# A cross-network kernel on one core: the first tile on two queues, a small product moved forward, and fewer pooling passes

## The chip, the cores and the metric

The kernel runs on one core of one Trainium2 chip. A core has a matrix engine (TensorE, "PE" in the profile; its weight loads are the row "PEld"), three engines for elementwise work (VectorE "DVE", ScalarE "ACT", GpSimd "POOL") and a queueing engine (SyncE, "SP"). SP, ACT and POOL can issue DMA transfers. The metric is the device time of one execution in microseconds; less is better.

## The reference

The reference is a compressed interaction network for recommendation, in float32. The input `x` has 1024 examples of 64 features by 16 embedding elements.

```python
x0 = h = x
for i in range(3):
    z = einsum('bfe,bge->bfge', x0, h).reshape(B, 64 * 64, e)
    y = einsum('oc,bce->boe', W[i], z) + b[i]
    x_i, h = (y[:, :64], y[:, 64:]) if i < 2 else (y, y)
    xs.append(x_i)
pooled = sum(concatenate(xs, axis=1), axis=2)
out = pooled @ fc_w.T + fc_b
```

Each layer forms all products of a feature of `x` with a feature of `h` and contracts them with weights; the last step pools over the 16 elements and weighs the channels to one number for each example. Since that step is linear, the kernel needs the third layer only through one weighted sum of its weights. So it builds a matrix "M" on the chip: layer 3's weights are summed with `fc_w` into `v2`, and M is `v2` times layer 2's upper weights. From M come the "Q weights", with which the same products z give a factor that is multiplied with `h` and pooled.

## The kernel before, in words

The work is cut into 32 chunks of 32 examples. A chunk's `x` is a tile of 512 columns (32 examples by 16 elements). The engine on the two sides of a product works on shifted copies of x: `xa` holds x with the features turned by 0 to 3 rows (4 slices, index i), `xb` holds x turned by multiples of 4 (4 quarters, index j). A product tile z for (j, i) is `xa[i] * xb[j]`, made by DVE or POOL (`product`, L239, whose instruction has line L243), and each z is contracted by TensorE with a 128 by 64 slice of `w_all`.

The program is written with a manual schedule: each engine runs its instructions in the order of the text, and semaphores are waited for where data is needed. The first four chunks ("head", c0 to c3, in the order 2, 3, 0, 1) run straight in program order; what follows is a list of operations with due times, sorted at L1075.

The order of the head is this.

- ACT issues the DMA of `vs` (L103), a tile of 128 by 196 with biases, factors and a column of `fc_w`. ACT makes `fv2` from it (L108), the weights of the `pv` matmuls.
- TensorE runs seven matmuls on zeros into the scratch bank `misc` (L113-114).
- SP issues x of c0 and the layer-1 weights slice by slice (L193-197; the instruction of `load_xa` has line L145), x of c1 (L198), layer 3's weights `w2t` (L202), layer 2's `w1h` (L203, L206), and c2's tiles.
- TensorE makes the shifted quarters of c0 and c1 by multiplying the first x slice with 0/1 matrices (`shift_pair`, L221, tiles "xp"). DVE, POOL and ACT make products and weights slice by slice; TensorE contracts c0 (L260).
- c1 is contracted in quarters by `half_contract` (L251). Between its quarters TensorE computes `pv` (L369), which DVE turns and ACT and DVE copy to `v2t` (L374 to L384).
- M is four matmul groups `pm` (L398) and a small one `pcx` (L407). ACT copies M to SBUF (L409). M is written to DRAM tile `md` by six DMAs (L421-431: two at L422, one each at L425, L426, L427, L428), on SP and one on ACT, and read back in two skewed patterns (L472, L478). `q_weights` (L505, DVE) adds both into the Q weights.
- c2 and c3 are contracted by L251, then `head_q_tile` (L284) contracts c0 and c1 with the Q weights.
- `linear` (L351-354) is a row of 384 numbers broadcast to 128 partitions by one DMA on SP. POOL multiplies parts of it (L456), DVE sums it (L969), into the constant of the output.

After the head, pairs of chunks follow the list of due times (matmuls at L536, products at L650 and L667). At the end, `acc` holds for each chunk pair k two parts of the pooled sums: part 0 from the factors, part 1 from `x_v0x`. `add_parts` (L1028) adds them for all pairs but k = 1, the last one, `pools` (L1034) sums over partitions by small matmuls `pool` (L952; the weights are two columns "ones") into `po`, and `finish` (L959) adds the constant and writes the result. The pair k = 1 is completed last, with weights `turned` that swap the two halves, and its last columns have a bank `pl` of their own.

Of the kernel before, what the change touches and what calls it, by code (L numbers as in the profile page):

```python
# [38 lines left out]
AF = mybir.ActivationFunctionType  # L39
# [7 lines left out]
N = CB * E  # L47
H2 = N // 2
CUT = 24
NCH = B // CB  # L50
NI = 4
NJ = 4
NT = NI * NJ
XR = 128 + NI
# [6 lines left out]
QS = 16.0  # L61
# [9 lines left out]
def cin_kernel(ctx, tc, xra, xrb, wh, w0r, w1h, w2t, wx1, wx0, vec, lin, out):  # L71
    nc = tc.nc
# [8 lines left out]
    def const_tile(name, shape):  # L81
        return const.tile(shape, F32, tag=name, name=name)
# [9 lines left out]
    def used(n, times=1):  # L92
        left[n] -= times
        assert left[n] >= 0
        if left[n] == 0:
            vacant.append(n)
# [3 lines left out]


    vs = const_tile("vs", [128, NV])
    nc.scalar.dma_start(out=vs, in_=vec)  # L103
    fc2, bh1, bh2 = vs[:, 0:1], vs[:, 1:2], vs[0:64, 2:3]
    fcb, w0ds, fcr = vs[:, 3:4], vs[:, 4:68], vs[:, 68:196]

    fv2 = const_tile("fv2", [128, 32])
    nc.scalar.activation(fv2, fc2.to_broadcast([128, 32]), AF.Identity, scale=QS)  # L108

    misc = ps.tile([128, N], F32, tag="acc", name="misc", bufs=4)  # L110

    zeros = nc.const_aps.tensor(0.0, [128, 128])
    for n in (128,) * 6 + (64,):  # L113
        nc.tensor.matmul(misc[:, 0:n], zeros, zeros[:, 0:n], start=True, stop=True)

    shift = const_tile("shift", [128, 96])
# [1 line left out]
    for base in (0, 64, -64):  # L118
        nc.gpsimd.affine_select(
            out=shift, in_=shift, compare_op=ALU.not_equal, fill=1.0, base=base,  # L120
# [18 lines left out]

    xas, xbs, xxs, es = {}, {}, {}, {}  # L140

    def load_xa(c, at=slice(0, NI)):
        if c not in xas or at.start == 0:
            xas[c] = xp.tile([128, NI, N], F32, tag="xa", name=f"xa_{c}")
        nc.sync.dma_start(  # L145
            out=xas[c][:, at, :],
            in_=bass.AP(
                tensor=xra.tensor, offset=c * XR * N + at.start * N,
                ap=[[N, 128], [1, (at.stop - at.start) * N]],
            ),  # L150
        )

    def quarter(c, j):
        xbs.setdefault(c, {})[j] = xp.tile([128, N], F32, tag="xb", name=f"xb_{c}_{j}", bufs=9)
        return xbs[c][j]
# [26 lines left out]
    def load_chunk(c):  # L182
        load_xa(c)
        load_xb(c)

    c0, c1, c2, c3 = HEAD
# [4 lines left out]
    w1b = take()  # L191
    w1s = flat(w1b)
    for i in range(NI):  # L193
        load_xa(c0, slice(i, i + 1))
        nc.sync.dma_start(out=w0t[:, i, :], in_=wh if i == 0 else w0r[:, i - 1, :])
        if i == 0:
            load_xa(c1, slice(0, 1))
    load_xa(c1, slice(1, 4))  # L198
    w0s = [w0t[:, i, :].rearrange("p (j v g) -> p j v g", v=2, g=F) for i in range(NI)]
    xb_gps = [quarter("gps", n) for n in range(3)]  # L200
    for k in range(2):
# [30 lines left out]
    acc = const_tile("acc", [128, 2, NCH // 2, CB])  # L232
# [15 lines left out]
    def half_contract(c, *js, last=None):  # L248
        for j in js:
            for i in range(NI):  # L250
                nc.tensor.matmul(  # L251
                    accs[c][halves[i % 2]], w_all[:, j * NI + i, 0:64], blocks[zs[c, j]][:, i, :],
                    start=(j == 0 and i < 2), stop=(j == last and i > 1),
                )
            used(zs[c, j])
# [12 lines left out]
    def keep_h1(c):  # L268
        if c != c0:
            h, k = halves[c % 2], c // 2  # L270
            nc.scalar.activation(hb[h, k, :], accs[c][halves[0]], AF.Identity, bias=bh1[halves[0]])
            nc.scalar.copy(snaps[k][h], accs[c][halves[1]])
            return
        for n in range(2):
            nc.scalar.activation(
                hb[halves[c % 2], c // 2, n * H2 : (n + 1) * H2], accs[c][halves[n]],
                AF.Identity, bias=bh1[halves[n]],
            )
# [53 lines left out]
    for i in range(NI):  # L332
# [15 lines left out]
    new_acc(c1)  # L348

    load_chunk(c3)  # L350
    linear = const_tile("linear", [128, 384])  # L351
    nc.sync.dma_start(
        out=linear, in_=bass.AP(tensor=lin.tensor, offset=lin.offset, ap=[[0, 128], [1, 384]])
    )
    keep_h1(c0)
    for j in (3, 2):
        product(c1, j, engine=nc.gpsimd)
# [8 lines left out]
    for n in range(2):  # L366
        pv = ps.tile([128, 512], F32, tag=("set", "y")[n], name=f"pv2_{n}")
        for k in range(4):
            nc.tensor.matmul(  # L369
                pv[32 * k : 32 * k + 32], fv2, w2s[n][:, k * 512 : (k + 1) * 512],  # L370
                start=True, stop=True,
# [9 lines left out]
    for h in range(2):  # L381
        at = slice(32 * h, 32 * h + 32)
        nc.vector.tensor_copy(v2t[halves[h], at], v2q[halves[h]])
        nc.scalar.copy(v2t[halves[1 - h], at], v2q[halves[h]])  # L384
    used(v2b)
    half_contract(c1, 1, 2, last=2)


    mb = take()
# [15 lines left out]
    pcx = ps.tile([128, 1], F32, tag="acc", name="pcx", bufs=4)  # L405
    for to in halves:
        nc.tensor.matmul(pcx[to], v2t[0:64], bh2, start=True, stop=True)  # L407
    for m in (0, 2, 1, 3):
        nc.scalar.copy(m_sb[:, m, :], pms[m])  # L409

# [5 lines left out]
    def m_ap(f1, f2, dims):  # L416
        return bass.AP(tensor=md.tensor, offset=md.offset + f1 * row + f2 * F, ap=dims)
# [3 lines left out]
    for half, queue in enumerate((nc.sync, nc.scalar)):  # L421
        queue.dma_start(  # L422
            out=m_ap(0, 32 * half, [[row, F], [1, 32 * F]]), in_=m_rows[halves[half]]
# [4 lines left out]
    nc.sync.dma_start(  # L428
        out=m_ap(64, 68, [[row, 4], [4 * F, 7], [1, 4 * F]]),
        in_=m_rows[0:4, 4 * F :].rearrange("p (k c) -> p k c", c=4 * F),  # L430
    )
    used(mb)

# [35 lines left out]
    queues = (nc.sync, nc.scalar)  # L469
# [47 lines left out]
    turned = const_tile("turned", [128, 2])  # L517
    for n in range(2):
        nc.gpsimd.memset(turned[halves[n], n : n + 1], 0.0)
        nc.gpsimd.memset(turned[halves[n], 1 - n : 2 - n], 1.0)  # L520
    nc.gpsimd.memset(acc[:, 0, 1, CUT:], 0.0)


    ops = []
# [1 line left out]
    def at(when, fn, *args, **flags):  # L526
        ops.append((when, len(ops), fn, args, flags))

    def zipped(when, *columns):
        for n, column in enumerate(columns):  # L530
            for m, job in enumerate(column):
                if job is not None:
                    at(when + m + n / len(columns), *job)
# [387 lines left out]
    for n, p in enumerate(pairs):  # L921
        t = T0 + SPAN * n
# [23 lines left out]
    NP = NCH // 2  # L946
    QP = NP // 4
# [4 lines left out]
    def pool(k0, k1, part=0, rows=ones, **flags):  # L952
        g, at = k0 // QP, slice(k0 % QP, (k1 - 1) % QP + 1)
        nc.tensor.matmul(  # L954
            po[0][32 * g : 32 * g + 2, at, :], rows, acc[:, part, k0:k1, :],
            tile_position=(0, 32 * g), skip_group_check=True, **flags,
        )

    def finish(k0, k1, queue):  # L959
        g, at = k0 // QP, slice(k0 % QP, (k1 - 1) % QP + 1)  # L960
        rows = slice(32 * g, 32 * g + 2)
        nc.scalar.activation(
            res[rows, at, :], po[0][rows, at, :], AF.Identity, bias=cst[rows]
        )
        queue.dma_start(out=outs[:, k0:k1, :], in_=res[rows, at, :])
# [14 lines left out]
    t, q = T0 + SPAN * NPAIR, pairs[-1]  # L980
    first, cuts = slice(0, CUT), (slice(0, E * CUT), slice(E * CUT, N))
# [32 lines left out]
    def end_uu(n):  # L1014
        cols = cuts[n]
        nc.vector.scalar_tensor_tensor(
            uu[:, 0, cols], ends[n], 1.0 / QS, snaps[3][:, cols], ALU.mult, ALU.mult
        )
# [6 lines left out]
    def quarters():  # L1025
        return [(0, 1), (2, QP)] + [(n, n + QP) for n in range(QP, NP, QP)]
# [5 lines left out]
        po.append(ps.tile([128, QP, CB], F32, tag="set", name="po"))  # L1032

    def pools():  # L1034
        for m in quarters():
            pool(*m, start=True, stop=True)
        pool(1, 2, 1, start=True, stop=False)
        for m in quarters():
            finish(*m, nc.sync)

# [8 lines left out]
    for when, c in ((-5, 2), (0, 3)):  # L1049
# [11 lines left out]
    at(t - 0.7, end_squares)  # L1061
    at(t + 9.9, end_h)
    at(t + 13.6, x_v0x, 1)
    at(t + 13.7, sums, 1, of=slice(1, 2))
    t += 23
    at(t - 8, add_parts)
    at(t - 0.2, end_uu, 0)
    at(t - 0.1, sums, 1, of=slice(0, 1), half=first)
    zipped(
        t,  # L1070
        *[[(end_q, c, m, 1) for m in range(NT)] + [(end_extra, c, 1)] for c in (3, 2)]
    )
    at(t + 8, pools)

    for when, n, fn, args, flags in sorted(ops, key=lambda op: op[:2]):  # L1075
# [2 lines left out]

    last = cuts[1]
    end_uu(1)  # L1080
    pool(1, 2, rows=turned, start=False, stop=True)
    pl = ps.tile([2, N - E * CUT], F32, tag="acc", name="pl", bufs=4)
    nc.tensor.matmul(pl, ones, uu[:, 1, last], start=True, stop=False)
    nc.tensor.matmul(
# [81 lines left out]
```

## Time and profile before

| what | value |
|---|---|
| three runs of the kernel before | 445.19, 444.74, 446.3 us (median 445.19) |
| the profiled execution | 444.88 us |
| its span, first to last instruction | 443.1 us |
| TensorE busy | 439.6 us (99%) |
| DVE busy | 402.2 us (91%) |
| POOL busy | 373.5 us (84%) |
| ACT busy | 117.7 us (27%) |
| first x tile landed | 4.05 us |
| last instruction of the output's DMA issue | 440.90 us |

Times inside the trace count from the first instruction of the span. A row of the timeline gives start, length, engine, line, operation, output tile and inputs, and the count of merged instructions, then the idle time of the engine before it and what ended it. A float32 matmul stands in the trace as two passes, so the seven matmuls on zeros are 14 rows. Matmuls on different parts of the array start together: a pair of 64-column matmuls, or four of 64 by 64, share one time slot. The ends of matmuls are modelled, so the distance from start to start tells the pace. The chain of work follows the end back through what released each step.

### The profile page before, as it was taken

To read this page: it belongs to the slowest core of one execution; us is meant where nothing else is said; L and a number is where in the kernel's file an instruction comes from. 1 tells how busy PE (TensorE), PEld (TensorE's weight loads), DVE (VectorE), ACT (ScalarE), POOL (GpSimd) and SP (SyncE) were. 2 spreads that over 40 slices of the span, in tenths; PEclk is the share of its full clock that TensorE was granted. 3 is DMA by queue.
4 is the path that set the end of the run, shared out by engine and by line. 5 is a ranking of instruction groups with operands and counts; after the bars stand their busy time and mean duration, and the time that the engine had idled before them with its cause. 6 is when DMAs were issued, how large, how long until landed. Compare 5 with 4: busy or idle time off the path is not lost.

```text
span 443.1 us, 5949 instructions
## 1 busy us (share of the span) xinstructions
PE 439.6 (99%) x2234; PEld 160.8 (36%) x2234; DVE 402.2 (91%) x305; ACT 117.7 (27%) x216; POOL 373.5 (84%) x136
## 2 busy tenths in 40 slices
PE   9999999999999999999999999999999999999997
PEld 5333344336533333333333333333333333333345
DVE  4896899999998999999999999999999999999744
ACT  3164341242412123131312314131231313123211
POOL 4916799999998979899898979989798997989900
PEclk9999999999999999999999999999999999999999
DMA  8998997399769756896849868597568958592400
GB/s 302 409 342 189 353 410 308 105 337 240 268 135 328 180 190 233 185 332 125 300 140 254 269 163 300 125 333 185 185 233 183 347 120 288 189 272 66 89 1 0
DMA packets 35204, 99.85 MB, mean 225 GB/s; under 512 B 6404, under 2 KB 7204, under 8 KB 28712
## 3 DMA queue, kind: packets, MB, share of 16 engines
q1 hardware_dynamic: 31704, 84.70, 53.9%
q0 software_dynamic: 1872, 13.63, 16.8%
q10 hardware_dynamic: 1600, 1.15, 1.1%
q8 instruction: 17, 0.28, 0.3%
q14 instruction: 11, 0.09, 0.1%
HBM read 84.20 MB, written 1.64 MB: 194 GB/s over the span
## 4 chain that ended last, share of the span: by engine, by line
PE 98%; DMA 1%; DVE 0%; issue 0%
PE alpha L536 43%; PE delta L536 23%; PE beta L536 11%; PE acc L536 7%; PE acc L251 5%; PE q L536 3%; PE acc L284 3%; PE acc L260 2%; PE xp L221 1%; DMA xa<-in_xra 1%; PE y L536 0%; PE pv L369 0%; PE pm L398 0%; PE hx L536 0%; PE po L954 0%; DVE hb L1091 0%
## 5 line engine op out<-in xcount | busy, mean ns | idle before, releaser
L667 POOL TENSOR_TENSOR z<-z,z 128x2048 f32<-128x2048 f32 (+1 forms) x85 | 300.2, 3576 | 24.4 <-PE alpha L536 13.9
L650 DVE TENSOR_TENSOR z<-xa,xp 128x2048 f32<-128x2048 f32 x103 | 231.3, 2280 | 2.9 <-ACT xp L564 1.0
L536 PE MATMUL alpha<-z,ws 128*64 128x512 f32 x624 | 233.3, 593 | 0.0
L536 PEld LDWEIGHTS alpha<-z,ws 128*64 128x64 f32 x624 | 74.5, 137 | 89.5 <-issue 81.9
L536 PE MATMUL delta<-z,w_all 128*64 128x512 f32 x208 | 96.4, 592 | 0.0
L536 PE MATMUL alpha<-z,w_all 128*64 128x512 f32 x208 | 92.4, 592 | 0.0
L536 PE MATMUL beta<-z,w_all 128*64 128x512 f32 x208 | 91.7, 594 | 0.0
L536 PE MATMUL delta<-z,ws 128*64 128x512 f32 x208 | 91.4, 592 | 0.0
L564 ACT COPY xp<-xb 128x512 f32<-128x512 f32 x88 | 51.4, 586 | 130.0 <-DVE z L650 112.9
L243 DVE TENSOR_TENSOR z<-xa,xp 128x2048 f32<-128x2048 f32 (+2 forms) x29 | 43.3, 1546 | 3.1 <-ACT xp L564 2.0
L536 PEld LDWEIGHTS alpha<-z,w_all 128*64 128x64 f32 x208 | 28.5, 137 | 29.1 <-issue 28.0
L536 PEld LDWEIGHTS delta<-z,w_all 128*64 128x64 f32 x208 | 28.5, 137 | 28.7 <-issue 27.4
L536 PEld LDWEIGHTS delta<-z,ws 128*64 128x64 f32 x208 | 28.5, 137 | 28.7 <-issue 27.4
L243 POOL TENSOR_TENSOR z<-xa,xb 128x2048 f32<-128x2048 f32 x6 | 27.2, 4553 | 13.6 <-DMA xb<-in_xrb 13.5
L536 PEld LDWEIGHTS beta<-z,w_all 128*64 128x64 f32 x208 | 28.0, 137 | 27.4 <-issue 25.7
L536 PE MATMUL acc<-z,w_all 128*64 128x512 f32 x128 | 28.2, 592 | 0.0
L681 ACT ACTIVATE snap<-alpha,vs 64x512 f32<-64x512 f32 x13 | 8.9, 683 | 52.1 <-PE alpha L536 52.1
L251 PE MATMUL acc<-z,w_all 128*64 128x512 f32 x96 | 21.4, 596 | 0.0
L308 DVE TENSOR_REDUCE acc<-uu 128x64 f32<-128x1024 f32 (+2 forms) x19 | 19.6, 1036 | 0.2
L684 ACT COPY snap<-delta 64x512 f32<-64x512 f32 x13 | 7.6, 581 | 42.2 <-PE alpha L536 27.7
L656 DVE TENSOR_TENSOR xp<-xp,xb 128x512 f32<-128x512 f32 x26 | 18.1, 697 | 0.6
L243 POOL TENSOR_TENSOR z<-xa,xb_gps 128x512 f32<-128x512 f32 (+1 forms) x6 | 14.1, 2380 | 5.0 <-ACT xb_gps L322 4.7
(129 smaller groups left out, 372.0 us busy)
## 6 DMA issues: line engine op xcount, KB each, us to landing
xa<-in_xra SPq DMA_DIRECT2D x32, 1024.0 KB, 5.8
xb<-in_xrb SPq DMA_DIRECT2D x128, 256.0 KB, 7.6
z<-z POOLq DMA_DIRECT2D x13, 1024.0 KB, 8.0
e<-in_xra SPq DMA_DIRECT2D x28, 128.0 KB, 7.3
xx<-in_xra SPq DMA_DIRECT2D x28, 128.0 KB, 2.5
z<-in_w2t SPq DMA_DIRECT2D x2, 1024.0 KB, 10.1
z<-in_wx SPq DMA_DIRECT2D x2, 1024.0 KB, 9.3
xa<-in_xra SPq DMA_DIRECT2D x5, 256.0 KB, 4.8
```

Of the source, the lines that this page charges most:

```text
L243: engine.tensor_tensor(blocks[zs[c, j]][:, at, :], xas[c][:, at, :], xbs[c][j].unsqueeze(1).to_broadcast([128, last - first, N]), ALU.mult,)
L251: nc.tensor.matmul(accs[c][halves[i % 2]], w_all[:, j * NI + i, 0:64], blocks[zs[c, j]][:, i, :], start=(j == 0 and i < 2), stop=(j == las ...
L260: nc.tensor.matmul(accs[c][halves[n]], w_all[:, j * NI + i, 0:64], blocks[zs[c, j]][:, i, n * H2 : (n + 1) * H2], start=(i == 0 and j == j ...
L284: nc.tensor.matmul(accs[c][halves[1 - c % 2]], w_all[:, t, 64:128], blocks[zs[c, j]][:, i, :], start=(t == 0), stop=False, skip_group_chec ...
L308: nc.vector.tensor_reduce(acc[rows, of, k, half], uu[rows, of if at is None else at, E * half.start : E * half.stop].rearrange("p k (b e) ...
L536: nc.tensor.matmul(out, w, rhs, start=start, stop=stop, skip_group_check=True)
L564: nc.scalar.copy(bank, xbs[c][j])
L650: engine.tensor_tensor(blocks[b], xas[c], xbs[c][j].unsqueeze(1).to_broadcast([128, NI, N]), ALU.mult)
L656: nc.vector.tensor_tensor(bank, bank, xbs[p["b"]][j], ALU.add)
L667: nc.gpsimd.tensor_tensor(*(blocks[b][:, first:last] for b in (o, x, y)), ALU.subtract if in1 == "T3" else ALU.add,)
L681: nc.scalar.activation(snaps[1][p["O"]], alpha(p), AF.Identity, bias=bh1[p["A"]])
L684: nc.scalar.copy(snaps[2][p["A"]], delta(p))
```

## The change

Five edits are made together.

1. The first x slice of c0 is loaded by two DMAs of 64 partitions each, one issued on SP and one on ACT. The DMA of `vs` goes from the head of ACT's queue to SP's queue, behind x of c1. `fv2` is made on ACT later, ahead of `keep_h1(c0)`.
2. The warm-up on zeros has six matmuls with 736 columns in all, where it had seven with 832.
3. M (`pm`, `pcx`) is computed after quarter 1 of c1's contraction; quarter 2 follows M.
4. The DMA of `linear` is issued behind M's six writes.
5. For k = 1 the two parts of `acc` change places, so that four pooling matmuls of equal size cover all pairs ahead of the end, and the completing matmul reads the other part.

```diff
-    nc.scalar.dma_start(out=vs, in_=vec)
...
-    for n in (128,) * 6 + (64,):
+    for n in (128,) * 5 + (96,):
         nc.tensor.matmul(misc[:, 0:n], zeros, zeros[:, 0:n], start=True, stop=True)
...
-    def load_xa(c, at=slice(0, NI)):
+    def load_xa(c, at=slice(0, NI), queues=(nc.sync,)):
...
+        rows = 128 // len(queues)
+        for n, queue in enumerate(queues):
+            queue.dma_start(
+                out=xas[c][rows * n : rows * (n + 1), at, :],
+                in_=bass.AP(
+                    tensor=xra.tensor, offset=c * XR * N + (at.start + rows * n) * N,
+                    ap=[[N, rows], [1, (at.stop - at.start) * N]],
+                ),
+            )
...
-        load_xa(c0, slice(i, i + 1))
+        load_xa(c0, slice(i, i + 1), (nc.sync, nc.scalar) if i == 0 else (nc.sync,))
...
     load_xa(c1, slice(1, 4))
+    nc.sync.dma_start(out=vs, in_=vec)
...
     load_chunk(c3)
-    linear = const_tile("linear", [128, 384])
-    nc.sync.dma_start(
-        out=linear, in_=bass.AP(tensor=lin.tensor, offset=lin.offset, ap=[[0, 128], [1, 384]])
-    )
+    fv2 = const_tile("fv2", [128, 32])
+    nc.scalar.activation(fv2, fc2.to_broadcast([128, 32]), AF.Identity, scale=QS)
     keep_h1(c0)
...
-    half_contract(c1, 1, 2, last=2)
+    half_contract(c1, 1)
...
         nc.tensor.matmul(pcx[to], v2t[0:64], bh2, start=True, stop=True)
+    half_contract(c1, 2, last=2)
     for m in (0, 2, 1, 3):
         nc.scalar.copy(m_sb[:, m, :], pms[m])
...
+    linear = const_tile("linear", [128, 384])
+    nc.sync.dma_start(
+        out=linear, in_=bass.AP(tensor=lin.tensor, offset=lin.offset, ap=[[0, 128], [1, 384]])
+    )
     used(mb)
...
-    nc.gpsimd.memset(acc[:, 0, 1, CUT:], 0.0)
+    nc.gpsimd.memset(acc[:, 1, 1, CUT:], 0.0)
...
     def pools():
-        for m in quarters():
-            pool(*m, start=True, stop=True)
-        pool(1, 2, 1, start=True, stop=False)
+        for k in range(0, NP, QP):
+            pool(k, k + QP, start=True, stop=k > 0)
...
-    at(t + 13.7, sums, 1, of=slice(1, 2))
+    at(t + 13.7, sums, 1, of=slice(0, 1), at=slice(1, 2))
...
-    at(t - 0.1, sums, 1, of=slice(0, 1), half=first)
+    at(t - 0.1, sums, 1, of=slice(1, 2), half=first, at=slice(0, 1))
...
-    pool(1, 2, rows=turned, start=False, stop=True)
+    pool(1, 2, 1, rows=turned, start=False, stop=True)
```

More of the change, by code (lines that the diff above doesn't have):

```diff
@@ L102, in cin_kernel @@
     vs = const_tile("vs", [128, NV])
-    nc.scalar.dma_start(out=vs, in_=vec)
     fc2, bh1, bh2 = vs[:, 0:1], vs[:, 1:2], vs[0:64, 2:3]
     fcb, w0ds, fcr = vs[:, 3:4], vs[:, 4:68], vs[:, 68:196]
-    fv2 = const_tile("fv2", [128, 32])
-    nc.scalar.activation(fv2, fc2.to_broadcast([128, 32]), AF.Identity, scale=QS)
     misc = ps.tile([128, N], F32, tag="acc", name="misc", bufs=4)
     zeros = nc.const_aps.tensor(0.0, [128, 128])
-    for n in (128,) * 6 + (64,):
+    for n in (128,) * 5 + (96,):
         nc.tensor.matmul(misc[:, 0:n], zeros, zeros[:, 0:n], start=True, stop=True)
@@ L140, in cin_kernel @@
     xas, xbs, xxs, es = {}, {}, {}, {}
-    def load_xa(c, at=slice(0, NI)):
+    def load_xa(c, at=slice(0, NI), queues=(nc.sync,)):
         if c not in xas or at.start == 0:
             xas[c] = xp.tile([128, NI, N], F32, tag="xa", name=f"xa_{c}")
-        nc.sync.dma_start(
[L146 to L150, printed above, removed]
-        )
+        rows = 128 // len(queues)
[7 more added lines that the diff above has]
+            )
     def quarter(c, j):
@@ L350, in cin_kernel @@
     load_chunk(c3)
-    linear = const_tile("linear", [128, 384])
-    nc.sync.dma_start(
-        out=linear, in_=bass.AP(tensor=lin.tensor, offset=lin.offset, ap=[[0, 128], [1, 384]])
-    )
+    fv2 = const_tile("fv2", [128, 32])
+    nc.scalar.activation(fv2, fc2.to_broadcast([128, 32]), AF.Identity, scale=QS)
     keep_h1(c0)
```

## The prediction

> **What bounds the kernel now.** I read the page's first table and chain, then the chain in order of time for the first 45 us, the waits between 30 and 48 us, and the single rows around every place where TensorE's rhythm breaks.
>
> ```profile
> PE 439.6 (99%) x2234; PEld 160.8 (36%) x2234; DVE 402.2 (91%) x305; ACT 117.7 (27%) x216; POOL 373.5 (84%) x136
> ...
> PE 98%; DMA 1%; DVE 0%; issue 0%
> ```
>
> TensorE is busy for 439.6 of 443.1 us and carries 98% of the chain. The chain by time says where the rest is:
>
> ```profile
> 0.75 3.30 DMA xa<-in_xra
> 4.05 0.14 issue
> 4.18 3.70 PE xp L221 x24
> 7.89 3.62 PE acc L260 x32
> ...
> 27.22 14.07 PE acc L251 x64
> ```
>
> One DMA, the first x tile, lands at 4.05; from 4.18 on TensorE never stops. Busy is not the same as on time, so I read the starts of its matmuls one by one. A 512-column pass of a pair of 64-column matmuls starts every 0.429 us all the way. Breaks: about 0.10 + 0.05 us at each change of tile shape (64*64, 128*32, 128*64), the first two passes, and two true waits, at 33.64 and at 40.69. So three kinds of change can move the end: TensorE starts earlier, has less to do, or waits less. What only makes another engine or a queue faster is worth nothing.
>
> **Start: first x in halves, vectors away.** Removed: the vectors' DMA (98 KB) on ACT's queue at 0.75, beside x. Added: one more DMA issue (ACT's half of x). Of 14 warm-up passes 12 are left.
>
> ```profile
> L221 PE MATMUL xp<-xa,shift x32: 589/612/1112, 4.2 to 11.9; 64*64 64x512 f32 x32
> ```
>
> The longest of these, 1112 ns against the usual 589, are the first ones: starts at 4.18, 5.06, 5.91, then every 0.43. TensorE still runs at half speed there; the granted clock is on record as full only from 6.05.
>
> How much earlier does x land? In the trace's DMA packets both queues begin at 1.78 and 1.86 us, and the same engines carry eight 2048-byte packets of x (84 ns each) and eight 784-byte packets of the vectors (38 ns each) interleaved. Without the vectors 8 x 0.038 = 0.30 us goes. The other end below: 0, if the start-up gaps between the first packets set the landing. Above: x alone at the later pace (the next 256 KB tiles land 0.65 us apart), so data from 1.86 to 2.51 and then the roughly 0.6 us from the last packet (3.45) to the semaphore (4.05): landing at 3.1, which the warm-up (below) cuts to some 0.7 us gained. I take 0.30, the count from packets. In cold time a pass costs 0.865 (mean of 0.877 and 0.853) for 0.429 of full-speed work, so 0.30 us earlier is worth 0.30 x 0.429 / 0.865 = **0.15 us**, with 0 and 0.35 as ends, and 0.7 if the full clock were already granted.
>
> The row on halves: before, one 128-row issue took 0.41 us on SP and the vectors' issue 0.40 on ACT, side by side, and their packets shared the engines. The Trainium skill's page "DMA: Bandwidth & Descriptors", section "Rules for kernel authors", speaks against this part: two transfers to disjoint partition halves share the same engines, so it advises one 128-partition transfer. By the rule the split itself gives nothing and only the absent vectors give the 0.15; if splitting and queueing cost what they save, the sum below loses up to 0.15.
>
> The warm-up's cover: its columns fall from 832 to 736, two passes each; 128 columns take 0.213, so it ends 2 x 96 x 0.213 / 128 = 0.32 us earlier, streaming to 3.37 instead of 3.69. x at 3.75 is still later, so the warm-up costs nothing; with the old length it would also have been covered.
>
> The vectors are next needed for fv2, which feeds the pv matmuls at 16.06. They now sit on SP's queue behind the second chunk's x, which landed at 12.07, so they land near 12.1. ACT runs fv2 (0.23 us) after its copy at 12.62, near 13.3. Slack 2.6 us; even a table load of 1.28 us in front of it (ACT's row at 1.18) stays covered. On SP the issue (0.4 us) goes ahead of w2, w1 and chunk 2; these are bound by bytes that arrive later than that (w2's first half landed at 14.56, 8.6 us after its issue), and the total of bytes ahead of them is the same.
>
> **M between the half contractions.** The same matmuls and the same number of shape changes (pv, four passes, pm, four passes instead of pv, eight, pm): 0 us on TensorE. M starts four passes earlier, 4 x 0.429 = 1.72 us: pm near 23.35 instead of 25.22. Its inputs: v2's last copy ends at 23.02 (less the start's 0.15), w1's second half landed at 23.72 and is wanted two passes into M, near 24.3. Slack 0.4 and 0.5 us; if either is gone, TensorE stalls by the excess. ACT's four copies (2.06 us) and then M's writes on SP and ACT move from 28.45 to some 26.6. Chunk 1's last matmuls now end near 27.0, and ACT's keep_h1 for it (30.78) comes long after.
>
> **Linear behind M's writes.** M's writes landed from 32.78 to 37.16 because chunk 3's loads and then linear (192 KB) were ahead of them on SP's queue (xb's last quarter at 30.87, linear at 31.35). Without linear the queue reaches M 0.48 us sooner, no more, since the loads stay. So M's chain gains about 0.5 us, not 1.9. Where that counts:
>
> ```profile
> 40.64 0.43 DVE L505 TENSOR_TENSOR w_all<-z 128x256 f32<-128x256 f32 x1 [1.60 <-DMA z<-md]
> 41.18 0.23 PEld L284 LDWEIGHTS acc<-z,w_all 128*64 128x64 f32 x4 [0.77 <-issue]
> 41.21 1.08 PE L284 MATMUL acc<-z,w_all 128*64 128x512 f32 x4
> ```
>
> DVE waits for M's way back, makes the first Q weights until 41.07, and TensorE, due at 41.12, starts at 41.21 with a slow first pass (0.521 and 0.452 for two 0.429): 0.09 + 0.02. If the start gave 0.15, TensorE is due at 40.97, and the weights are there near 40.6 to 40.8. The wait goes: **0.12 us**. Ends: 0.12 above; below, -0.15, the start's gain given back here if the weights come no earlier. Linear is wanted by POOL at 36.86; it lands near 37.3, so POOL may wait 0.5 us. Cover: POOL idles 3.72 us before L863 a little later. The wait at 33.64 (TensorE for DVE's product, 0.14 + 0.05) stays: DVE runs without a gap from 22.95 to 34.15 and is itself released by pv, so both shift together.
>
> **Pooling.** Six matmuls (12 passes) become four (8 passes) ahead of the end; add_parts, finish and the sums only change places.
>
> ```profile
> 437.23 0.41 PE L954 MATMUL po<-acc,ones 128*2 128x32 f32 x12
> 437.57 1.85 PE L536 MATMUL q<-z,w_all 128*64 128x128 f32 x29
> ```
>
> From 437.23 to the return to q are 0.336 us: first passes within 0.03, the last start at 0.196, 0.140 after that. With four equal groups side by side the second passes start near 0.12 and q follows near 0.27: **0.07 us** less, ends 0 and 0.11. The tail behind the last q is released by DVE (L1016) and unchanged.
>
> **Sum.** 0.15 + 0.12 + 0.07 = 0.34. The profiled execution took 444.88 (span 443.1 and 1.8 around it): 444.88 - 0.34 = 444.54, so **444.5**. The three runs have a median of 445.19, 0.31 above the profiled one, and spread over 1.56; the range carries that. Below 0.3% (1.33 us) a measurement of this kernel can't tell a change from none.
>
> The Trainium skill's page "TensorE: Matmul & The Clock Gate", section "Part 1: The HAM clock gate", says that the activity window runs freely, so the release point differs from run to run; one trace can't show that, but it would make part of that spread.
>
> **Rivals.**
> *The gain is given back at the Q weights.* M's way through DRAM is bound by the queue, so linear's leaving could be eaten by linear's own bytes, now ahead of the reads (192 KB, 0.49 us at the measured pace). For it: DVE is late already. Against: the queue is idle from 37.2 to 38.0. Then TensorE starts L284 at 41.21 as before: 444.88 - 0.07 = 444.8.
> *M's write collides with chunk 3's last quarter (slower).* ACT's half of M's write is issued near 26.6 while xb streams until 30.87, and POOL waits for that very quarter:
>
> ```profile
> POOL z L243 <- DMA xb<-in_xrb: 9.8, 1, 9.8
> ...
> PEld acc L251 <- DVE z L243: 1.6, 3, 0.8
> PEld acc L251 <- POOL z L243: 0.4, 1, 0.4
> ```
>
> POOL's product ends at 35.66, TensorE takes it at 35.97: 0.31 us of slack. ACT's write needs 2.5 us of the engines (32.0 to 34.5). If all of it went in front of xb, POOL ends at 38.16, and TensorE, due at 35.82, stalls 2.34 + 0.05: 444.88 + 2.39 - 0.15 - 0.07 = 447.05. It decides from 0.3 us of delay on. Against it, DMA between 29.5 and 31.9:
>
> ```profile
> q1 hardware_dynamic: 111, 0.59, 110.3%
> ```
>
> Only SP's queue moved, although ACT's write had been issued at 28.45: it began at 32.0, behind SP's half. Issued earlier it should queue again.
> *The start gains more:* x 0.7 us earlier at full clock, both waits gone, 0.11 from pooling: 0.7 + 0.12 + 0.19 + 0.11 = 1.12, so 443.8.
> *It doesn't do what it says:* x lands when it did; the halves wait for each other: 444.88 - 0.19 = 444.7.
>
> **Numbers.** Forecast 0.57, given back 0.15, no earlier x 0.13, more 0.08, collision in some size 0.07. The range, 443.9 to 445.7, goes from near the "more" case to the median's offset and a small collision. Faster by over 0.3% needs the "more" case and a fast median, 0.05; slower is the collision, 0.06; within 0.89.
>
> **What would show it.** Start: xp's first matmul near 3.88, acc L260 near 7.67. M: pm near 23.35, M's ACT copies near 24.5, ACT's packets still behind SP's; L284 with no 0.52 pass and starting near 40.95. Pool phase 0.27. Wrong: a POOL product of chunk 3 starting after 31.3, a stall ahead of pm, pv late for fv2, or a cold stretch that lasts longer than until 6.05.

## The result, and the profile after

| | before | after |
|---|---|---|
| median of 22 runs each | 445.23 us | 446.79 us |
| lowest and highest | 444.57 to 446.85 | 444.51 to 450.84 |
| runs above 447 us | 0 of 22 | 11 of 22 |
| profiled execution (span) | 444.88 (443.1) | 446.03 (444.2) |

The ratio of after to before is 1.0036, with a 95% interval of 1.0019 to 1.0052: the change makes the kernel slower by 0.36%, and the forecast (444.5, at most 445.7) missed it. The lowest run is as fast as the lowest before; what is new is a group of runs at 447 to 451. The time is lost in two places, and the profiled execution, one of the lower group, shows only the first.

**Place one: POOL's product of chunk 3.** The page of after gives TensorE the same busy time as before and a smaller part of the chain:

```profile
PE 439.7 (99%) x2228; PEld 158.0 (36%) x2228; DVE 402.7 (91%) x305; ACT 117.7 (26%) x216; POOL 373.9 (84%) x136
...
PE 91%; DMA 6%; POOL 1%; SPq 1%; issue 0%; DVE 0%; POOLq 0%
```

The chain in order of time (start, length, what) has the rest:

```profile
4.93 5.44 DMA z<-in_w0r
10.37 0.02 issue
10.38 13.95 DMA z<-in_w1h
...
24.40 8.05 DMA xb<-in_xrb
...
32.67 4.57 POOL z L242
37.24 0.04 issue
37.28 5.37 PE acc L250 x24
42.66 13.73 PE acc L283 x64
```

Before, TensorE alone carried the chain from 4.18 on, and one unbroken row went from 27.22 to 41.29. Now the chain runs through the loads up to 37.28. Quarter 3 of chunk 3's xb is issued when w1's second half has landed, at 24.40 (23.79 before), and lands at 32.45 (30.87), so POOL's product ran at 32.67 instead of 31.09. The row of the kernel before:

```profile
31.09 4.56 POOL L243 TENSOR_TENSOR z<-xa,xb 128x2048 f32<-128x2048 f32 x1 [9.81 <-DMA xb<-in_xrb]
```

The issue is 0.61 us late, the way from issue to landing 0.97 us longer. The waits of after between 30 and 48 us (total, times, longest) say the same:

```profile
POOL z L242 <- DMA xb<-in_xrb: 11.2, 1, 11.2
...
PE acc L250 <- POOL z L242: 1.1, 1, 1.1
```

POOL's wait grew from 9.8 to 11.2 us. TensorE, which before had 0.31 us of slack, started its pass at 37.28 where its rhythm asked for 35.98. That is 1.30 us; the span grew by 1.1. These are the DMA packets of after between 29.5 and 31.9 us (packets, MB, share of 16 engines):

```profile
q1 hardware_dynamic: 122, 0.53, 56.0%
q10 hardware_dynamic: 49, 0.40, 50.9%
```

Before, this window had q1 alone. q10 is ACT's queue, and its 0.40 MB are M's write, in packets of 8192 bytes (309 to 646 ns each, the first at 30.43) beside xb's 2048-byte packets (about 84 ns). A DMA lands in 16 shares; 15 of the quarter's were in by 30.43, the last came at 32.45. The price of 1.30 us is that of one execution: of the kernels below, the one with `add_h1` on POOL, which is the same as after up to this point, lost 0.70 us here, and the one with linear back 0.25.

**The rest of the profile.** The first matmul on x starts at 3.66 (4.18 before), the contraction of c0 at 7.34 (7.82). Between kernels this stretch varies with the clock by more than that (last section). But xb of chunk 2 landed at 23.04 (22.43 before), DVE waited 0.43 us for it, and at 33.66 TensorE waits for DVE as it did at 33.64: nothing of the start is left by then. The slow first pass with the Q weights (0.52 us at 40.69 before) is gone. The pooling phase goes from 438.45 to 438.79, 0.33 us with eight passes, where twelve took 0.336.

```profile
438.45 0.40 PE L956 MATMUL po<-acc,ones 128*2 128x128 f32 x8
438.79 1.85 PE L538 MATMUL q<-z,w_all 128*64 128x128 f32 x29
```

These are two rows of the timeline of after. Behind its 128-column groups 0.20 us pass from the last start to the return to q, where behind the 32-column ones it was 0.14. What fewer passes save, wider ones spend.

### The profile page after: what moved, and what is told of

It is laid out like the page before. It is cut to its first block, busy times and chain, and to the rows that moved or that the text cites. A ratio compares the mean times of both kernels' runs of the same rounds, so it can differ in the third digit from the quotient of the medians.

```text
span 444.2 us, 5939 instructions
## 1 busy us (share of the span) xinstructions
PE 439.7 (99%) x2228; PEld 158.0 (36%) x2228; DVE 402.7 (91%) x305; ACT 117.7 (26%) x216; POOL 373.9 (84%) x136
## 4 chain that ended last, share of the span: by engine, by line
PE 91%; DMA 6%; POOL 1%; SPq 1%; issue 0%; DVE 0%; POOLq 0%
PE alpha L538 43%; PE delta L538 23%; PE beta L538 11%; PE acc L538 7%; PE q L538 3%; DMA z<-in_w1h 3%; PE acc L283 3%; DMA xb<-in_xrb 2%; DMA z<-in_w0r 1%; PE acc L250 1%; POOL z L242 1%; SPq L143 1%; PE y L538 0%; SPq L193 0%; PE hx L538 0%
```

## The experiments

Each kernel was run 11 or 12 times, beside runs of the kernel before on the same chip. "Above 447" counts runs. The kernel before has 2 of 163 runs there.

| kernel | median | before beside it | ratio (95%) | above 447 |
|---|---|---|---|---|
| M alone | 445.04 | 444.98 | 1.0000 (0.9992 to 1.0009) | 0 of 11 |
| after, M back | 445.40 | 444.98 | 1.0017 (1.0000 to 1.0035) | 1 of 11 |
| after, M's write all on SP | 445.43 | 444.98 | 1.0028 (1.0005 to 1.0052) | 4 of 12 |
| after, quarter 3 first | 444.74 | 444.98 | 1.0019 (0.9998 to 1.0039) | 3 of 12 |
| the same, add_h1 on POOL | 444.68 | 445.09 | 0.9990 (0.9982 to 0.9999) | 0 of 12 |
| start alone (edits 1, 2) | 445.17 | 445.09 | 1.0003 (0.9993 to 1.0013) | 0 of 12 |
| linear alone (edit 4) | 445.25 | 445.09 | 1.0009 (0.9991 to 1.0027) | 3 of 12 |
| after, linear back | 445.58 | 445.09 | 1.0010 (1.0000 to 1.0021) | 0 of 12 |
| after, add_h1 on POOL | 445.24 | 444.94 | 1.0007 (0.9998 to 1.0016) | 0 of 11 |
| after, linear back, quarter 3 first | 444.76 | 444.94 | 0.9999 (0.9990 to 1.0008) | 0 of 11 |
| before, quarter 3 first, add_h1 on POOL | 444.93 | 444.94 | 1.0001 (0.9993 to 1.0010) | 0 of 11 |
| start alone, vectors on ACT | 445.43 | 444.94 | 1.0009 (1.0001 to 1.0018) | 0 of 11 |
| quarter 3 first, linear ahead of the last write | 444.86 | 445.03 | 0.9999 (0.9986 to 1.0013) | 2 of 12 |
| quarter 3 first, linear back, tiny DMA late | 444.40 | 445.03 | 0.9983 (0.9970 to 0.9995) | 0 of 11 |
| quarter 3 first, last read on SP | 445.16 | 445.20 | 1.0004 (0.9995 to 1.0013) | 0 of 11 |

The first theory had one place: M's early write on ACT's queue delays quarter 3. Its rival: the later load stream delays it, whatever M does.

**M alone** (the kernel before with edit 3):

```diff
-    half_contract(c1, 1, 2, last=2)
+    half_contract(c1, 1)
...
+    half_contract(c1, 2, last=2)
```

> The kernel before with M between c1's quarters and nothing else. Collision theory (M's writes, issued 1.9 us earlier, share the DMA engines with the last quarter of chunk 3's xb; its slowest share lands late, POOL's product of it is late, TensorE waits): POOL's product starts after 31.4, a TensorE gap of 0.3 to 1.5 us ahead of that quarter, median 445.6 to 447 with single runs over 447. Late-stream theory (the vectors and the second issue of x in SP's stream make all of chunk 3 land 0.6 us later, and that alone is the loss): 445.0 to 445.4, no run over 447.

POOL's product started at 31.64, with a stall of 0.60 us at 35.24, inside the expected 0.3 to 1.5. But the median stayed at 445.04: M's move alone does not slow the kernel. The part of the theory that gave it the whole loss fell.

**After with M back** (the reverse diff on after):

> The changed kernel with M back behind both quarters of c1. Collision theory: M's writes start behind chunk 3's loads again, 444.7 to 445.3, spread as before (under 2.5 us). Late-stream theory: POOL's product still starts near 31.7, a gap of 0.3 to 0.4 us stays and the median is 445.5 or more.

POOL's product started at 31.73 and TensorE lost 0.35 us at 35.58. So M alone, and the other edits alone, each delay the quarter by 0.55 to 0.64 us in their profiles; together they gave 1.58. One run of 11 came at 449.68, which the collision at quarter 3 can't explain here.

**M's write all on SP:**

```diff
-    for half, queue in enumerate((nc.sync, nc.scalar)):
+    for half, queue in enumerate((nc.sync, nc.sync)):
```

> The changed kernel with ACT's half of M's write issued on SP instead, so that on every DMA engine it stands behind chunk 3's loads in one queue. Collision theory with ACT's queue as the culprit: the last quarter lands near 31.0 to 31.4, gap under 0.4 us, 444.6 to 445.2, small spread; if M's chain grows by the lost overlap, L283 waits up to 1 us. If SP's own M writes are the culprit: as the change, 446 to 447. Late-stream theory alone: 445.5 to 446.

The quarter was in time (product at 30.97, stall 0.19). This alone is one profile, and its whole load stream was early (chunk 2's first quarter landed at 22.31). All profiles together say more: compare how far the last share of the quarter that is loaded last trails its middle share with the same in the quarter before it. In seven of the ten profiles with M's write issued on ACT by 27.0 us it trails 0.29 to 0.97 us further, in the other three no further; of the seven profiles with that write later or on SP, none does. So M's early write on ACT's queue makes the straggling share, though not in every execution. Yet four of 12 runs lie above 447: there is a second place. This profile touches it too: the second addition of `add_h1` (explained next) took 4.91 us beside POOL's product, though TensorE lost only 0.21 us.

**Quarter 3 first:**

```diff
-    load_chunk(c3)
+    load_xa(c3)
+    load_xb(c3, 3, 0, 1, 2)
```

> The changed kernel with chunk 3's quarter 3, POOL's, loaded ahead of quarters 0, 1, 2. Collision and late-stream theories both: POOL's product starts near 29.6, the gap ahead of quarter 3 is gone, and the quarter that now stands last (2) is wanted only at 36.27: 444.3 to 444.9, small spread, faster than both kernels. If the loss is in the start or in the clock and not at this quarter: 446 to 447 as the change.

Eight runs took 444.44 to 445.15, four 446.6 to 448.67. The product started at 29.39 and place one is cured. The profiled run, 448.34, fell into the second group and shows **place two**. First DVE, then POOL, by the timeline from 44 us (start, length, engine and line, then idle time before it and what ended it):

```profile
47.30 0.42 DVE L508 TENSOR_TENSOR w_all<-z 128x256 f32<-128x256 f32 x1 [4.00 <-DMA z<-md]
47.79 0.11 DVE L857 MEMSET w_all<- 32x64 f32 x1
47.93 6.72 DVE L978 TENSOR_TENSOR hb<-hb,snap 64x512 f32<-64x512 f32 x2
```

```profile
47.89 4.53 POOL L242 TENSOR_TENSOR z<-xa,xb 128x2048 f32<-128x2048 f32 x1 [2.25 <-PE acc L283]
```

M's last read, on ACT's queue, landed at 47.20 (42.7 to 45.0 in all profiles but four), so the last Q weights came at 47.30. Behind them in program order stand the two additions of `add_h1`. In the kernel before they took 0.69 us each, and POOL's product came behind them (DVE, then POOL):

```profile
47.07 1.41 DVE L975 TENSOR_TENSOR hb<-hb,snap 64x512 f32<-64x512 f32 x2
```

```profile
49.63 4.56 POOL L243 TENSOR_TENSOR z<-xa,xb 128x2048 f32<-128x2048 f32 x1 [3.06 <-DMA xb<-in_xrb]
```

Here POOL's product starts 0.04 us ahead of them, and the first takes 5.04 us, until 0.55 us past the product's end; the second takes 1.65. Then DVE's product for chunk 4 is late, and TensorE waits for it (waits, same kernel); by the starts of its matmuls it loses 2.69 us at 54.12:

```profile
PE acc L539 <- DVE z L242: 2.5, 1, 2.5
```

The Trainium skill's page "SBUF — State Buffer", section "SBUF: two separate sides", says that a GpSimd operation that reads SBUF and a VectorE operation with two inputs in SBUF exclude each other for the whole instruction. The 5.04 us agree with it; DVE's products with the shifted copies `xp`, which lie in PSUM, keep to 2.29 us beside POOL's product (from 49.23 in the next kernel).

**The same with add_h1 on POOL:**

```diff
-            nc.vector.tensor_tensor(hb[h, k, :], hb[h, k, :], snaps[k][h], ALU.add)
+            nc.gpsimd.tensor_tensor(hb[h, k, :], hb[h, k, :], snaps[k][h], ALU.add)
```

> The changed kernel with quarter 3 of chunk 3 loaded first and the two additions of add_h1 moved from DVE to POOL. Theory (a DVE addition beside POOL's product takes 5.0 us instead of 0.7 and holds up the product that TensorE waits for): on POOL it can't run beside POOL's product, so the stall of 2.7 us near 54 us goes, the median is 444.4 to 444.7 and no run is above 446.2. Rival (the late return of M delays TensorE by itself, through the Q weights): a quarter of the runs stay at 446.5 or more, as with the quarter alone (4 of 12).

No run lies above 445.21, and the interval of the ratio (0.9982 to 0.9999) lies just under 1. Its profile is a clean test, since M's last read was just as late (DVE, then POOL):

```profile
47.39 0.43 DVE L508 TENSOR_TENSOR w_all<-z 128x256 f32<-128x256 f32 x1 [2.44 <-DMA z<-md]
...
49.23 8.97 DVE L242 TENSOR_TENSOR z<-xa,xp 128x2048 f32<-128x2048 f32 x4 [0.78 <-ACT xp L567]
```

```profile
46.16 2.79 POOL L978 TENSOR_TENSOR hb<-hb,snap 64x512 f32<-64x512 f32 x2
48.92 4.57 POOL L242 TENSOR_TENSOR z<-xa,xb 128x2048 f32<-128x2048 f32 x1
```

The Q weights come at 47.39, later than in the kernel that stalled, and TensorE does not stall there: the profiled run took 444.89. The late read cost nothing by itself. It costs when it puts the additions beside POOL's product.

**Start alone**, the kernel before with edits 1 and 2:

> The kernel before with edits 1 and 2 alone (halves, vectors on SP behind chunk 1, shorter warm-up). Theory: x earlier by 0.1 to 0.4 us at the start, the later loads 0.3 to 0.6 us late, the start's gain given back at POOL's product of chunk 3: median 444.7 to 445.2, no run above 446.2, since M returns as before. Rival (the start, through the clock or the late loads, makes the runs of 447 to 450): at least 1 run in 12 above 446.5.

No run above 446.2. In the profile POOL's product was 0.45 us late without cost, against the theory, but the Q weights were now late: DVE made the first ones at 41.66 and TensorE lost 0.69 us at 41.12. There was no gain to give back in this execution: its full clock came only at 7.08 us, and c0's contraction began at 8.29 (7.82 before).

**Linear alone**, the kernel before with edit 4:

```diff
-    linear = const_tile("linear", [128, 384])
...
+    linear = const_tile("linear", [128, 384])
```

> The kernel before with edit 4 alone (linear behind M's writes). Theory A (linear's 192 KB in front of M's reads makes the last read straggle, add_h1 falls beside POOL's product): 1 to 4 runs of 12 above 446.5, median 445 to 445.3. Theory B (M's early reads beside chunk 4's loads make it, not linear): no run above 446.2, median 444.8 to 445.2. In both POOL waits 1 to 2 us for linear near 38 us.

Three of 12 runs took 447.23 to 447.87, as theory A expected. The profiled run (445.01) was not one of them: in it the last read landed at 44.29 and the additions took 0.69 us each.

**After with linear back** (the reverse diff on after):

> The changed kernel with linear back in front of M (edit 4 undone). Theory A (linear late makes the slow runs): no run above 447.5, the stall of 0.5 to 1.3 us at chunk 3's last quarter stays, median 445.2 to 446.2. Theory B (M early makes them): still 2 to 4 of 12 above 447.5. POOL's wait for linear goes in both.

None of 12 above 446.4, again theory A. The median lies 1.2 us under after's, which ran on another chip, so that distance is not the price of linear. The stall at quarter 3 was 0.25 us in its profile.

**After with add_h1 on POOL** and nothing else:

> The changed kernel with add_h1 on POOL and nothing else. Theory (two places: the late share of chunk 3's last quarter costs 0.3 to 1.5 us, the slowed DVE additions make the runs of 447 to 450): the stall near 35.6 us stays, the runs above 447 go, median 444.9 to 446.0. Rival (one place: whatever makes the quarter late also makes the slow runs, so only the quarter's order cures): at least 2 runs in 12 above 447.

The runs above 447 are gone, and the stall at quarter 3 stayed (0.70 us at 35.35). The two places are separate.

**Linear back and quarter 3 first:**

> The changed kernel with linear back in front of M (edit 4 undone) and quarter 3 of chunk 3 loaded first. Theory (linear behind M's writes is what pushes the return of M into the slow additions; the quarter's order cures the other place): no stall near 35.6 us, no run above 446.2, median 444.4 to 444.8, with add_h1 still on DVE. Rival (M's earlier reads make the slow additions too): at least 2 runs in 12 above 446.5.

As the theory expected, with the additions still on DVE: no run above 445.13, and no stall of TensorE near 35.6 us.

**The kernel before with both cures:**

> The kernel before with the same two cures (quarter 3 first, add_h1 on POOL) and none of the five edits. If the five edits are worth something once both places are cured, this stays at 444.9 to 445.2, above the 444.68 of the changed kernel with the cures. If they are worth nothing and the cures are all, it comes to 444.5 to 444.8 as well.

It stayed at 444.93, ratio 1.0001: on the kernel before, the cures gain nothing. They need not be free there: in its profile TensorE lost 0.43 us at 33.21, waiting for DVE.

**Start alone with the vectors on ACT's queue:**

```diff
+        if i == 0:
+            nc.scalar.dma_start(out=vs, in_=vec)
...
-    nc.sync.dma_start(out=vs, in_=vec)
```

> Edits 1 and 2 alone, as before, but the vectors' DMA stays on ACT's queue, behind its half of x. Theory (the vectors' place on SP's queue, one more issue and 98 KB behind chunk 1, makes the later loads 0.4 to 0.7 us late): chunk 2's and 3's quarters land within 0.2 us of the kernel before (xb's first quarter of chunk 2 at 22.4 to 22.6), median 444.7 to 445.0. Rival (the halves themselves are late, through issues of 0.57 us in place of 0.41): the quarters stay 0.4 us or more late, median 445.0 to 445.3.

The trace went with the theory: chunk 2's first quarter landed at 22.53 (22.84 with the vectors on SP, 22.43 before), chunk 3's last at 31.01 (31.32, 30.87). But such a difference is within the spread of single profiles: chunk 2's first quarter landed between 22.31 and 23.29 in the twelve kernels with the vectors on SP (mean 22.93) and between 22.30 and 22.83 in the four with the old start (mean 22.56). That the vectors' place makes the stream late is likely by the means, and not shown by this run. The time did not follow: 445.43. In the profile TensorE lost 0.24 us at 35.18 for POOL's product and 0.26 us at 40.61 for Q weights made at 40.73. So an earlier stream alone was worth nothing while M returns as before.

Why does linear behind M's writes make M's last read late? Theory S: in its new place ACT's fourth read of M gets a DMA semaphore that ACT's first one still uses; in seven profiles it started 0.02 to 0.03 us after that one had landed. Theory B: its 192 KB, just ahead of the reads.

**Linear one place earlier**, ahead of M's last write, without that shared semaphore:

> The changed kernel with quarter 3 first, linear still late, but one place earlier in SP's queue: ahead of M's last write (28 KB) in place of behind it. In the traces so far with linear behind all writes, ACT's fourth read of M starts 0.02 to 0.03 us after ACT's first read has landed on the same semaphore; in this order the program has no such wait. Theory S (the shared semaphore makes the slow runs): ACT's reads are issued 0.7 us apart as before, no run above 446.5, median 444.5 to 444.8. Theory B (linear's 192 KB close ahead of the reads makes them): 2 or more of 12 runs above 446.5, as with quarter 3 first alone (4 of 12).

Two of 12 runs at 448, the profiled one among them. ACT's last read still came late, now behind the second one's semaphore (landed 41.03, issued 41.05). DVE and POOL by the timeline:

```profile
48.74 5.62 DVE L978 TENSOR_TENSOR hb<-hb,snap 64x512 f32<-64x512 f32 x2
```

```profile
48.74 5.06 POOL L242 TENSOR_TENSOR z<-xa,xb 128x2048 f32<-128x2048 f32 x1 [2.66 <-DVE w_all L857]
```

**Linear early, a DMA of 4 bytes in its late place**, with the shared semaphore:

```diff
+    spare = const_tile("spare", [128, 1])
+    nc.sync.dma_start(out=spare[0:1], in_=bass.AP(tensor=lin.tensor, offset=lin.offset, ap=[[0, 1], [1, 1]]))
```

> The changed kernel with quarter 3 first and linear early, and one extra DMA of 4 bytes at linear's late place, behind M's writes. It moves no bytes, but gives ACT's fourth read of M the same wait for ACT's first one. Theory S (the shared semaphore): the fourth read is issued 1.3 us or more after the third, and 2 or more of 12 runs are above 446.5. Theory B (linear's bytes): no run above 446.5, median 444.6 to 444.9.

No run above 444.87. ACT's fourth read again started right behind the first one's landing, but that landing took 2.40 us from its issue (3.54 with quarter 3 first alone), so the wait was 0.31 us. Theory S alone falls. In the profile that took 448.34 us (quarter 3 first) the first read landed late and the shared semaphore handed the lateness on; that linear's bytes made it late is the reading that is left, not one shown by itself (with linear late and M back, the first read took 2.41 us). This kernel has the lowest median of the study. Why it lies under the one with linear back and quarter 3 first (another chip, 444.76) wasn't tested.

**M's last read on SP's queue:**

```diff
-            read_columns(j, queue, half)
+            read_columns(j, nc.sync if j == NJ - 1 else queue, half)
```

> The changed kernel with quarter 3 first, linear late and the shared semaphore as in the change; only M's very last read goes from ACT's queue to SP's, where chunk 4's loads (8 KB and 2 KB packets) stand behind it. In the slow profiles that last read was issued within 0.7 us of chunk 4's first load and landed at 45.8 to 48.0. Theory (on ACT's queue its last packets wait beside chunk 4's loads): the read lands by 44.5, add_h1 takes 0.7 us an operation, no run above 446.5, median 444.4 to 444.8, though POOL still waits 1 to 3 us for linear. Rival (linear's bytes hold up the whole return of M, whichever queue the last read is on): 2 or more of 12 runs stay above 446.5.

The read landed at 44.51, the additions took 0.69 us each, no run lies above 445.74, and POOL still waited 1.85 us for linear. With linear's bytes unchanged, the runs above 446.5 are gone: what decides is that chunk 4's loads can no longer overtake the read. The median was expected at 444.4 to 444.8 and came to 445.16; its profile has the full clock only from 6.82, which may be part of that. The DMA queues between 43 and 47 us, with the last read on ACT (quarter 3 first), then on SP:

```profile
q1 hardware_dynamic: 371, 1.28, 92.0%
q10 hardware_dynamic: 59, 0.01, 1.6%
```

```profile
q1 hardware_dynamic: 375, 1.33, 90.3%
```

In the first, ACT's read drips at 3 to 14 packets of 256 bytes per half microsecond. A packet takes 15 to 18 ns even so; the time goes in the gaps between them, while chunk 4's 8192-byte packets run (309 ns at the median, 355 on average). The Trainium skill's page "DMA: Bandwidth & Descriptors", section "Queues, rings and completion order", has each DMA engine take turns between the queues packet by packet. That fits the drip, and the straggling quarter in place one, where the large packets were on ACT's queue and the small ones on SP's. Whether the page's packets are the packets of the trace, no run here shows.

In the profiles, ACT's last read landed after 45.5 us where chunk 4's first load was issued within 0.7 us of it or before it (four kernels), and by 45.0 where 0.98 us or more lay between.

## Why the prediction was wrong

- **Linear at zero: the step that failed.** The working asked who waits for linear (POOL, covered) and what M gains. It did not count linear's 192 KB as bytes ahead of M's reads except in a rival, which let them cost only the Q weights' gain. All kernels with linear late, `add_h1` on DVE and the last read on ACT have 24 of 81 runs above 447 (quarter 3 first or not); the kernels of the table with linear early have 0 of 79, and those with linear late but add_h1 on POOL or the last read on SP 0 of 34. DVE's work behind the Q weights was not followed to the point where `add_h1` meets POOL's product: there TensorE lost 2.69 us (quarter 3 first, at 54.12) and 1.46 us (linear ahead of the last write, at 55.05). POOL's own wait for linear, forecast at 0.5 us, came to 1.1 to 1.9 us in six profiles, still covered.
- **The collision at quarter 3: right in kind, 0.07 in chance.** The argument against it failed: that ACT's write, issued earlier, "should queue again" behind SP's half. Its packets ran from 30.43 us, while xb was still coming. The price was 1.30 us in the profile of after and 0.70 in that of a kernel that is the same up to there, of the 2.34 written, and M's move alone is only part of it. That the median of 446.79 lies near this rival's 447.05 is chance, since most of the runs that raise it belong to the other place.
- **That "the total of bytes ahead of them is the same": failed.** The vectors behind chunk 1 and the longer issues of the halves stand in front of w1's second half and of chunk 2's and chunk 3's quarters. These landed about 0.6 us later in the profile of after; over all profiles with this start chunk 2's first quarter came 0.37 us later on average, and which of the two causes it is was not separated. In after it cost 0.26 us at pm, the start's gain at DVE, and part of the slack at quarter 3.
- **Start, 0.15:** the first matmul came 0.52 us earlier, and none of it reached 33.66. Alone, the start gave 1.0003 and 1.0009. With the vectors on ACT 0.34 us of it reached 33.30 and was given back, half at POOL's product and half at the Q weights. The second half is what the first rival foretold, but linear, which that rival blamed, was not moved in this kernel. The warm-up, said to cost nothing, was the bound in nine of the thirteen profiles with this start: x's first half landed at 3.28 to 3.47, and the first matmul followed the warm-up at 3.56 to 3.60.
- **Q weights, 0.12:** the short stall went, as forecast. In after the 1.30 us lost ahead of it would have hidden it, but it is gone with M alone and in most of the kernels with quarter 3 first as well (with linear ahead of the last write TensorE lost 0.34 us there). The reason given was wrong. The working let M's chain gain only 0.5 us, by linear's leaving. M's reads began 1.65 us earlier in after, 1.71 with M alone and 0.53 with linear alone, so M's own move gave most of it.
- **Pooling, 0.07:** 0.00 to 0.01. The return to q was mis-sized: 0.20 us behind a 128-column pass, not 0.14.
- With both places cured the ratio is 1.0004, 0.9999, 0.9990 or 0.9983, that is from 0.2 us more to 0.8 us less. The forecast's 0.34 lies inside, and so does nothing at all: the sizes of the gains are not settled. The queues were not followed.

That linear's new place sets after's own upper group is shown by the counts; no execution of after in that group was profiled.

## What to carry to other kernels

When a DMA is moved, list what is behind it in its new place, on every queue that shares the DMA engines, and follow each to the engine that waits for it; in both places here the transfer of small packets beside one of large packets on another queue was the one that came late. When a wait gets later, look at what the waiting engine does next, and whether another engine that excludes it is then at work. Look at the spread of the runs as well as at one profile: the profiled execution of the change showed one cause of two.

## What the runs showed beyond that

- The point where the full clock is granted ranged from 4.19 to 7.08 us in profiles of kernels with the same warm-up (5.6, 6.44, 6.61 and 6.82 among those between), and c0's contraction began anywhere from 6.92 to 8.29. This is more than the start's whole forecast gain.
- A DMA of 64 partitions took 0.57 to 0.61 us to issue at the start, against 0.41 for one of 128. The shape need not be the reason: the next DMA on SP, of 128 partitions, took 0.57 there too (0.44 before). But the half that came first (3.52) let TensorE begin on it alone, while the second half landed at 3.96, hardly before the whole tile (4.05).
- DVE's additions beside POOL's product: 5.04, 4.91 and 4.90 us for 0.69.
- Of the eight runs above 448.5 us in all kernels, seven have a mean granted clock of 0.996; every other run has 0.999 or 1.0. Over 447 us, 0.4% is about 1.8 us (an estimate from these two numbers), so these seven carry a stretch of lower clock besides the stall. Which of the two brings the other is not shown, since no such run was profiled.
